# Layer 0 of a fused four-layer kernel: VectorE's order, one stored copy of q*v for even images, unpadded blocks, and GpSimd on half of the product

## The chip, the cores and the metric

The kernel runs on one core of a Trainium2 chip. A core has TensorE (PE: matrix products, with a queue PEld for loading weights), VectorE (DVE), ScalarE (ACT), GpSimd (POOL), SyncE (SP, which here only issues DMAs) and 16 DMA engines. Each engine takes its own instructions in the order in which they stand, and waits at semaphores for the others. On-chip memory (SBUF) has 128 partitions; products arrive in PSUM, which has 8 banks. The metric is the device time in microseconds of one execution, as a median over runs.

## The reference

The whole reference is four layers on x of 8 images, 56 x 56 positions and 192 channels, each with a group norm ahead of it and a residual sum behind it. Only layer 0 matters here:

```python
p = silu(x @ p_w.T + p_b)
q = silu(x @ q_w.T + q_b)
v = silu(x @ v_w.T + v_b)             # 576 channels each
a1, a2 = mlp1(pos) * decay, mlp2(pos) * decay
qv = q * v
o1 = toeplitz(qv along w, a1)
o2 = toeplitz(qv along h, a2)
out = (p * (o1 + o2)) @ o_w.T + o_b
```

For each image and channel, `o1 + o2` is a product of q*v (56 x 56) with a Toeplitz matrix of 56 lags from the right, plus one with another Toeplitz matrix from the left. Both are done as one product whose summed dimension holds the rows of q*v and the rows of the Toeplitz matrix, alternately.

## The kernel before, in words

**Steps.** Layer 0 has two steps, and layers 1 to 3 follow. Step one is the loop over the images `for b in range(nimg)` with `layer0_in` and `layer0_qv`. Step two is `layer0_mix`, which multiplies with the Toeplitz rows and does the gate and the output projection. What passes from one to the other goes through two DRAM tensors, `left` and `right`. `left` holds q*v as (image, sub, h) rows of 56 x 64 (w, channel), `right` holds it as (image, sub, w) rows of (h, channel); a sub is 64 of the 576 channels. Behind q*v each holds the Toeplitz rows, 64 for each sub, of which the last 8 are zeros.

**Step one.** x lies as 128 partitions: 64 channels of one half of the image (s = 0) and 64 of the other (s = 1), three channel groups j and 1568 positions (`NH`) in each half. `layer0_in` takes the statistics (L157, twelve instructions an image), sums them over groups with two small matmuls (L176), takes a square root on ACT and normalises into `xn` (L371). `layer0_qv` goes over 14 tiles of 112 positions; for each, over two halves n of the channels (called half tiles here). A half tile is 12 matmuls (L387; in float32 each leaves two records, so 24), two sums with the bias on DVE (L393, from PSUM to `act`), two Silu on ACT (L394) and two products q*v on DVE (L395). `act` has 4 buffers, PSUM 4 tiles of two banks, `qv` 3 buffers. After both halves SP stores q*v: for each s one DMA to `left` (L398) and two to `right` (L403), all in pieces of 64 floats, 256 B.

**Between the tiles** the list `between[i]` runs other work: `coefs`, a generator that makes the Toeplitz coefficients in image 0 (L227 and on: two MLPs, small matmuls, DVE); `rows`, DMAs on ACT's queue that write the Toeplitz rows and the zero rows into `left` and `right` (L296, L301); `bias` and `masks` for layer 1 (bias table, L342 sums on DVE, DMAs on POOL's queue); `centred`, which prepares weights of layer 1 in image 2; and in tile 4 all of `layer0_in` of the next image.

**Order.** Nothing in step one is pinned: the framework's scheduler puts the instructions of each engine in an order by its own estimate of times, and may move work of a later image ahead of an earlier one.

**Step two.** For each image and sub a block is loaded by `layer0_block` (L417): `lt` and `rt`, 128 partitions of 56 x 64 floats, in which q*v rows and Toeplitz rows alternate; two buffers each, so the next block's load starts when the last but one is copied out. `layer0_operand` (L425) copies 8 or 16 channels out of it at a time: `lc` on POOL, `rc` on DVE and ACT in turn. `layer0_products` (L433) does 16 (or 8) small products from them: a group. A block is four groups (or eight smaller ones). In between, the gate (`layer0_gate`, L445 to L474; `layer0_gate_last`) of the preceding channels runs: projection p, Silu, transposes of o, product and output projection. One image is nine blocks.

Of the kernel before, what the change touches and what calls it, by code (L numbers as in the profile page):

```python
# [18 lines left out]
NT = H * W  # L19
# [43 lines left out]
NH = NT // 2  # L63
NTH = NH // TT
# [25 lines left out]
def kernel(ctx: ExitStack, tc: tile.TileContext, a: dict, out: bass.AP):  # L90
# [45 lines left out]
    none = dram.tile([QR], F32, name="none")  # L136
    left, right = (dram.tile([(nimg * W + 64) * NSUB, QR], F32, name=n) for n in ("left", "right"))
    qv_row = lambda b, s: (b * NSUB + s) * W
    toep_row = lambda s: nimg * NSUB * W + 64 * s
    x1 = [dram.tile([C, NT], F32, name=f"x1_{b}") for b in range(nimg)]  # L140
# [86 lines left out]
    def toeplitz_rows(psum, pool, rows):  # L227
# [62 lines left out]
        zero = pool.tile([128, QR // 128], F32, name="zero", bufs=1)  # L290
        nc.gpsimd.memset(zero, 0.0)
        nc.scalar.dma_start(none.rearrange("(p n) -> p n", p=128), zero)
        parts = [z[toep_row(0):].rearrange("(s k) n -> k s n", k=64) for z in (left, right)]
# [6 lines left out]
        def zeros(i, k):  # L300
            nc.scalar.dma_start(parts[i][k], none.partition_broadcast(NSUB))  # L301

        rows += [lambda i=i, k=k: zeros(i, k) for i in range(2) for k in range(W, 64)]
# [54 lines left out]
    def layer0_in(b, x, pool, psum):  # L358

        sc, sh = scsh[:, 0, b:b + 1], scsh[:, 1, b:b + 1]  # L360
        st = pool.tile([128, 3, NTH, 6], F32, name="gh_st")
        for t in range(NTH):
            gn_piece(st, x, t)
        mv = pool.tile([128, 1, 2], F32, name="gh_mv")
        gn_aggregate(st, mv[:, 0])
        run(gn_finish(mv, sc, sh, pool, psum, "qv"))
        xn = pool.tile([128, 3, NH], F32, name="xn0")
        n = NH if b else TT
        for t in range(NH // n):
            ts = bass.ts(t, n)  # L370
            nc.vector.tensor_scalar(xn[:, :, ts], x[:, :, ts], sc, sh, ALU.mult, ALU.add)  # L371
        return xn

    def layer0_qv(b, xn, pool, psum, w_qv, b_qv, between):

        lv, rv = (
            z[qv_row(b, 0):qv_row(b, 0) + NSUB * W].rearrange("(s h) (w d) -> s h w d", h=W, d=64) for z in (left, right)
        )
        for i in range(PH):
            qv = pool.tile([2 * W, 2, D1], F32, name="qv", bufs=3)  # L380
            for n in range(2):
                ns = slice(n * D1 // 2, (n + 1) * D1 // 2)
                ps = [psum.tile([2 * W, 2, 512], F32, name=f"qv{s}", tag="qv") for s in range(2)]
                for which in range(2):
                    for j in range(3):
                        for s in range(2):
                            nc.tensor.matmul(  # L387
                                ps[s][:, which, 0:D1 // 2], xn[64 * s:64 * s + 64, j, bass.ts(i, 2 * W)],
                                w_qv[64 * s:64 * s + 64, j, which, ns], start=(j == 0), stop=(j == 2),
                            )  # L390
                for s in range(2):
                    act = pool.tile([2 * W, 2, D1 // 2], F32, name="act", bufs=4)
                    nc.vector.tensor_tensor(act, ps[s][:, :, 0:D1 // 2], b_qv[:, :, ns], ALU.add)  # L393
                    nc.scalar.activation(act, act, AF.Silu)  # L394
                    nc.vector.tensor_tensor(qv[:, s, ns], act[:, 0], act[:, 1], ALU.mult)  # L395
            for s in range(2):
                h0 = H // 2 * s + 2 * i
                nc.sync.dma_start(  # L398
                    lv[:, h0:h0 + 2].rearrange("s h w d -> (h w) s d"),
                    qv[:, s].rearrange("t (s d) -> t s d", d=64),  # L400
                )
                for r in range(2):
                    nc.sync.dma_start(  # L403
                        rv[:, :, h0 + r].rearrange("s w d -> w s d"),
                        qv[r * W:(r + 1) * W, s].rearrange("w (s d) -> w s d", d=64),
                    )
            for step in between[i]:
                step()
# [1275 lines left out]
```

## Time and profile before

The profile is of one execution. Step one runs from about 28 to 849 us, step two to about 2050, layers 1 to 3 after that.

| what | value |
|---|---|
| median of 3 runs | 5769.45 us (5760.73 to 5771.72) |
| the profiled execution | 5770.6 us, its span 5768.8 us |
| busy over the span | PE 5181.2 us (90%), DVE 3336.5, ACT 2169.1, POOL 1420.2 |
| mean granted PE clock | 0.957 |
| `left` stores (L398) | 224 DMAs of 252 KB |
| `right` stores (L403) | 448 DMAs of 126 KB |
| block loads (L417) | 72 of `lt` and 72 of `rt`, 1792 KB each |
| DVE's q*v (L395) | 448 x 455 ns |
| ACT's Silu (L394) | 448 x 683 ns |
| DVE's normalisation (L371) of images 1 to 7 | 7 x 2729 ns |
| POOL's copies `lc` of 16 channels (L425) | 256 x 1936 ns |

How to read it: "busy" is the time in which an engine works on something, "records" are instructions as the profiler saw them. A group of instructions is named by line, engine, operation and tiles, then count, busy time, mean duration, and the idle time just before it with the name of what ended it. A view of stretches gives the busy time of each engine in that piece of the span; PE's clock in it is a share of the full one.

### The profile page before, as it was taken

The page shows a single profiled execution, that of the slowest core. Times are in us where ns is not written, and L with a number is a line of the kernel's source. Part 1 is how long each engine was busy: PE and PEld are TensorE (multiplying, and loading weights), DVE is VectorE, ACT ScalarE, POOL GpSimd, SP SyncE. Part 2 cuts the span into 40 slices and gives each one's busy share as a digit, 9 for nine tenths or more (in the row PEclk, how much of TensorE's full clock was granted, in tenths as well). Part 3 has the DMA queues.
Part 4 walks back from the last instruction along what each step waited for, and adds up shares of the span by engine and source line. Part 5 has one row for each costly group of instructions (what it writes and reads, how often), then busy time and mean ns, then how long its engine had stood idle before and what let it go on. Part 6 is the DMA issues. An engine that isn't in the chain of part 4 may idle for free. (4 is left out here: it accounts for less than half of the span.)

```text
span 5768.8 us, 116138 instructions
## 1 busy us (share of the span) xinstructions
PE 5181.2 (90%) x50342; PEld 3376.1 (59%) x50342; DVE 3336.5 (58%) x4710; ACT 2169.1 (38%) x2908; POOL 1420.2 (25%) x1107
## 2 busy tenths in 40 slices
PE   6898998999899979999997989999788798999999
PEld 4568765666666645555554657676344597444444
DVE  5777774555555546566665868888778202433331
ACT  2333443333333423333332004555476400433333
POOL 2100004444444424433342013333101101100100
PEclk8999999999999989999998989999899899999999
DMA  6888986776677633222222866666687598212211
GB/s 179 204 211 216 206 182 258 264 264 258 247 262 264 222 92 82 69 75 76 69 65 76 260 235 218 227 232 209 160 232 215 222 328 295 78 62 77 76 41 26
DMA packets 721922, 1013.94 MB, mean 176 GB/s; under 512 B 486376, under 2 KB 645444, under 8 KB 694644
## 3 DMA queue, kind: packets, MB, share of 16 engines
q1 hardware_dynamic: 706352, 940.12, 52.4%
q0 software_dynamic: 8512, 40.62, 2.1%
q10 hardware_dynamic: 6548, 25.78, 1.4%
q8 instruction: 396, 6.49, 0.5%
q14 instruction: 114, 0.93, 0.0%
HBM read 676.92 MB, written 345.97 MB: 177 GB/s over the span
## 5 line engine op out<-in xcount | busy, mean ns | idle before, releaser
L387 PE MATMUL qv<-w_qv_sb,xn 64*112 64x288 f32 x5376 | 711.3, 421 | 48.6 <-DVE act L393 45.4
L425 POOL COPY lc<-lt 128x896 f32<-128x896 f32 (+1 forms) x320 | 552.5, 1751 | 640.9 <-PE op L433 543.1
L387 PEld LDWEIGHTS qv<-w_qv_sb,xn 64*112 64x112 f32 x5376 | 558.5, 182 | 195.5 <-DVE act L393 58.1
L394 ACT ACTIVATE act<-act 112x576 f32<-112x576 f32 x448 | 300.6, 683 | 466.8 <-DVE act L393 427.4
L433 PE MATMUL op<-rc,lc 128*56 128x56 f32 x9216 | 339.1, 221 | 102.1 <-POOL lc L425 64.9
L433 PEld LDWEIGHTS op<-rc,lc 128*56 128x56 f32 x9216 | 307.8, 135 | 177.9 <-POOL lc L425 103.5
L1289 PE MATMUL ph<-y,w_sb 64*128 64x392 f32 x2304 | 397.7, 497 | 6.5 <-ACT hid L1293 6.5
L1300 PE MATMUL po<-hid,w_sb 128*64 128x392 f32 x2304 | 386.3, 494 | 0.0
L393 DVE TENSOR_TENSOR act<-qv,b_qv 112x576 f32<-112x576 f32 x448 | 320.7, 752 | 92.7 <-PE qv L387 92.4
L1307 DVE TENSOR_TENSOR x<-x,z 128x392 f32<-128x392 f32 x96 | 67.0, 698 | 524.2 <-ACT z L1305 524.2
L425 ACT COPY rc<-rt 128x896 f32<-128x896 f32 (+1 forms) x160 | 256.3, 1606 | 249.7 <-PE op L433 227.2
L805 PE MATMUL qk_ps<-xr,wg 64*96 64x392 f32 x1536 | 334.2, 538 | 1.8 <-DVE xr L752 1.7
L1016 PE MATMUL cv<-zc,wt 128*128 128x224 f32 x1536 | 313.6, 356 | 24.2 <-DMA zc<-pd 24.2
L1016 PEld LDWEIGHTS cv<-zc,wt 128*128 128x128 f32 x1536 | 291.0, 190 | 67.5 <-issue 51.2
L1289 PEld LDWEIGHTS ph<-y,w_sb 64*128 64x128 f32 x2304 | 220.0, 188 | 175.9 <-issue 25.5
L445 PE MATMUL pj<-xn,w_p_sb 64*128 64x392 f32 x1536 | 309.8, 511 | 12.4 <-DVE xn L533 8.2
L1190 PE MATMUL cps<-zc,wt 128*128 128x224 f32 x1536 | 300.2, 356 | 18.2 <-DMA zc<-zd 16.8
L1190 PEld LDWEIGHTS cps<-zc,wt 128*128 128x128 f32 x1536 | 289.6, 189 | 28.7 <-issue 21.3
L466 PE MATMUL y<-pp,w_o_sb 128*64 128x392 f32 x1536 | 285.9, 501 | 4.8 <-DVE x L474 4.1
L459 DVE TENSOR_TENSOR pp<-pp,ot 128x784 f32<-128x784 f32 x128 | 124.2, 970 | 284.8 <-ACT pp L450 272.9
L1300 PEld LDWEIGHTS po<-hid,w_sb 128*64 128x64 f32 x2304 | 162.7, 137 | 213.8 <-issue 213.8
L1031 POOL TENSOR_TENSOR rows<-rows,loc 128x896 f32<-128x896 f32 x96 | 220.8, 2300 | 261.7 <-ACT rows L1027 201.9
(233 smaller groups left out, 8895.1 us busy)
## 6 DMA issues: line engine op xcount, KB each, us to landing
lt<-left SPq DMA_DIRECT2D x72, 1792.0 KB
rt<-right SPq DMA_DIRECT2D x72, 1792.0 KB
left<-qv SPq DMA_DIRECT2D x224, 252.0 KB
right<-qv SPq DMA_DIRECT2D x448, 126.0 KB
wt<-in_band_dram SPq DMA_DIRECT2D x23, 2048.0 KB
wt<-in_band_dram SPq DMA_DIRECT2D x11, 4096.0 KB
zc<-pd SPq DMA_DIRECT2D x187, 232.0 KB
pd<-pt SPq DMA_DIRECT2D x7, 5568.0 KB
```

What stands on the lines that cost most here:

```text
L387: nc.tensor.matmul(ps[s][:, which, 0:D1 // 2], xn[64 * s:64 * s + 64, j, bass.ts(i, 2 * W)], w_qv[64 * s:64 * s + 64, j, which, ns], start ...
L393: nc.vector.tensor_tensor(act, ps[s][:, :, 0:D1 // 2], b_qv[:, :, ns], ALU.add)
L394: nc.scalar.activation(act, act, AF.Silu)
L425: copy(c[:, 0:nu], raw.rearrange("p (w u d) -> p u d w", u=nu, d=64 // nu)[:, :, d0:d0 + 8])
L433: nc.tensor.matmul(op[64 * u:64 * u + W, i, :], lc[:, u, i], rc[:, u, i], start=True, stop=True)
L445: nc.tensor.matmul(ps[0:M, s, 0:TT], w_p[64 * s:64 * s + 64, j, d0:d0 + M], xn[64 * s:64 * s + 64, j, ts], start=(j == 0), stop=(j == 2),)
L466: nc.tensor.matmul(y[64 * s:64 * s + 64], w_o[0:M, c, 64 * j:64 * j + 64], pp[0:M, s], start=(c == gated[0][0]), stop=(c == gated[-1][0]),)
L805: nc.tensor.matmul(in_pairs(ps[s]), wg[64 * s:64 * s + 64, j, c0:c0 + HC], in_slots(xr[64 * s:64 * s + 64], (3 * g + j) * GW), start=(j == ...
L1016: nc.tensor.matmul(dst, wt[:, c4 + i, 128 * q:128 * q + 128], zc[:, :, c4 + i, q:q + NPAIR], start=(q == 0), stop=(q == 1),)
L1190: nc.tensor.matmul(dst.rearrange("p (b n) -> p b n", n=NPAIR), wt[:, c4 + i, q * OP:(q + 1) * OP], zc[:, :, c4 + i, q:q + NPAIR], start=(q ...
L1289: nc.tensor.matmul(ps[:, s, 0:TT], w0[64 * s:64 * s + 64, j, m * 128:(m + 1) * 128], y[64 * s:64 * s + 64, j, ts], start=(j == 0), stop=(j ...
L1300: nc.tensor.matmul(ps[64 * s:64 * s + 64], w1[:, m, 64 * j:64 * j + 64], hid[:, m, s], start=(m == 0), stop=(m == 5),)
```

## The change

- **DVE in source order.** A manual schedule for DVE is entered before step one's loop, so that DVE's instructions stand as the program writes them. The first step of `coefs` is drawn ahead of the first `layer0_in`.
- **`layer0_in` is a generator.** It yields between statistics, the group sums and the normalisation; the loop draws one step after each of the tiles 3 to the last but one. Normalisation is done in four pieces, for image 0 on DVE and for the others on POOL.
- **`layer0_qv`**: even images have 13 tiles (twelve of 120 positions and one of 128), odd ones the 14 of 112. The products q*v of a half tile are written down after the bias sums of the next one; s = 0 on DVE and s = 1 on POOL.
- **Stores**: q*v of every image goes to `left`; only odd images also go to `right`, which is half as large.
- **Blocks**: `lt` and `rt` take 112 partitions, 56 rows of each kind in alternation, without the 8 pad rows. For an odd image `rt` comes from `right` as before. For an even one the Toeplitz rows come from `right` in one DMA and q*v from `left` in another, which turns (h, w) into (w, h) in pieces of 256 B.
- The zero rows and their 16 DMAs are gone.

```diff
+QT = [[(120 * i, 120) for i in range(12)] + [(1440, 128)], [(112 * i, 112) for i in range(14)]]
...
-    left, right = (dram.tile([(nimg * W + 64) * NSUB, QR], F32, name=n) for n in ("left", "right"))
+    left, right = (dram.tile([n * NSUB, QR], F32, name=z) for n, z in ((nimg * W + 64, "left"), (nimg // 2 * W + 64, "right")))
+    right_row = lambda b, s: 64 * NSUB + qv_row(b // 2, s)
...
-        rows += [lambda i=i, k=k: zeros(i, k) for i in range(2) for k in range(W, 64)]
...
+        xn = pool.tile([128, 3, NH], F32, name="xn0")
+        yield xn
         for t in range(NTH):
             gn_piece(st, x, t)
+            yield
         mv = pool.tile([128, 1, 2], F32, name="gh_mv")
         gn_aggregate(st, mv[:, 0])
-        run(gn_finish(mv, sc, sh, pool, psum, "qv"))
+        for _ in gn_finish(mv, sc, sh, pool, psum, "qv"):
+            yield
+        yield
+        for t in range(NTH):
+            ts = bass.ts(t, TT)
+            eng = nc.gpsimd if b else nc.vector
+            eng.tensor_scalar(xn[:, :, ts], x[:, :, ts], sc, sh, ALU.mult, ALU.add)
+            if t % 2:
+                yield
...
+        def multiply(i, t0, M, n, qv, acts):
+            ns = slice(n * D1 // 2, (n + 1) * D1 // 2)
+            for s in range(2):
+                eng = (nc.vector, nc.gpsimd)[s]
+                eng.tensor_tensor(qv[0:M, s, ns], acts[s][0:M, 0], acts[s][0:M, 1], ALU.mult)
+            for s in range(2 * n):
+                nc.sync.dma_start(
+                    bass.AP(one.tensor, one.offset + 64 * (NH * s + t0), [[64, M], [64 * NT, NSUB], [1, 64]]),
+                    qv[0:M, s].rearrange("t (s d) -> t s d", d=64),
+                )
+                for r in range(2 * (b % 2)):
+                    nc.sync.dma_start(
+                        rv[:, :, H // 2 * s + 2 * i + r].rearrange("s w d -> w s d"),
+                        qv[r * W:(r + 1) * W, s].rearrange("w (s d) -> w s d", d=64),
+                    )
+
+        for i, (t0, M) in enumerate(QT[b % 2]):
...
                 for s in range(2):
-                    act = pool.tile([2 * W, 2, D1 // 2], F32, name="act", bufs=4)
-                    nc.vector.tensor_tensor(act, ps[s][:, :, 0:D1 // 2], b_qv[:, :, ns], ALU.add)
-                    nc.scalar.activation(act, act, AF.Silu)
-                    nc.vector.tensor_tensor(qv[:, s, ns], act[:, 0], act[:, 1], ALU.mult)
+                    nc.vector.tensor_tensor(acts[s][0:M], ps[s][0:M, :, 0:D1 // 2], b_qv[0:M, :, ns], ALU.add)
+                for s in range(2):
+                    nc.scalar.activation(acts[s][0:M], acts[s][0:M], AF.Silu)
+                if later:
+                    later.pop()()
+                later.append(lambda now=(i, t0, M, n, qv, acts): multiply(*now))
...
+        x = left[qv_row(b, s):qv_row(b, s) + W]
+        twos = lambda one, delta: bass.AP(one.tensor, one.offset, [[QR, W], [delta * QR, 2], [1, QR]])
+        nc.sync.dma_start(raw[0][0:2 * W], twos(x, toep_row(s) - qv_row(b, s)))
+        rows_t, rows_x = 64 * s, right_row(b, s)
+        if b % 2:
+            nc.sync.dma_start(raw[1][0:2 * W], twos(right[rows_t:rows_t + W], rows_x - rows_t))
+        else:
+            nc.sync.dma_start(raw[1][0:2 * W:2], right[rows_t:rows_t + W])
             nc.sync.dma_start(
-                t, bass.AP(one.tensor, one.offset, [[QR, 64], [(odd - even) * QR, 2], [1, QR]]),
+                raw[1][1:2 * W:2].rearrange("w (h d) -> w h d", d=64), x.rearrange("h (w d) -> w h d", d=64)
             )
...
+        st.enter_context(tc.manual_schedule(engines={mybir.EngineType.DVE}))
+        next(coefs)
+        ahead = layer0_in(0, x, pool, psum)
+        xn = next(ahead)
+        run(ahead)
...
+                ahead = layer0_in(b + 1, x, pool, psum)
+                xn_next = next(ahead)
+                for i in range(3, len(QT[b % 2]) - 1):
+                    between[i].append(lambda: next(ahead, None))
             layer0_qv(b, xn, pool, psum, w_qv, b_qv, between)
-            xn = ahead[0] if ahead else None
+            run(ahead)
+            xn = xn_next
```

## The prediction

> **What bounds the kernel now.** First the groups of instructions by cost, for step one (q, v and q*v of the eight images) and step two (the products with the Toeplitz rows).
>
> ```profile
> L387 PE MATMUL qv<-w_qv_sb,xn 64*112 64x288 f32 x5376 | 711.3, 421 | 48.6 <-DVE act L393 45.4
> ...
> L393 DVE TENSOR_TENSOR act<-qv,b_qv 112x576 f32<-112x576 f32 x448 | 320.7, 752 | 92.7 <-PE qv L387 92.4
> ...
> L433 PE MATMUL op<-rc,lc 128*56 128x56 f32 x9216 | 339.1, 221 | 102.1 <-POOL lc L425 64.9
> ```
>
> Step one's products start at 28.6 us and its last activation is at 848.6: 820 us. Step two reads what step one left in DRAM, and its products start at 854, so a microsecond gained in step one is gained at the end. Second, the busy time in stretches of 20 us: span, PE, PEld, DVE, ACT and POOL busy (with instructions), granted clock, DMA share, GB/s.
>
> ```profile
> 60.00:80.00 20.00, 11.81 (x64) 7.94 (x66) 15.25 (x35) 4.06 (x6) 0.00 (x0) 0.67 0.64 153
> ...
> 500.00:520.00 20.00, 20.00 (x168) 20.00 (x166) 15.69 (x28) 9.45 (x14) 0.00 (x0) 1.00 0.97 220
> ...
> 540.00:560.00 20.00, 10.83 (x65) 10.14 (x63) 12.52 (x25) 3.72 (x7) 0.00 (x0) 0.74 0.66 179
> ...
> 620.00:640.00 20.00, 17.98 (x133) 13.30 (x131) 15.15 (x28) 9.78 (x14) 0.00 (x0) 0.91 0.96 237
> ...
> 760.00:780.00 20.00, 20.00 (x170) 14.81 (x168) 16.17 (x28) 9.44 (x14) 0.00 (x0) 1.00 0.87 178
> ```
>
> Undisturbed, PE does 168 records in 20 us, 8.4 per us, at clock 1.00: 5376 records would take 640 us. The other 180 us are the stretches like 60 and 540, with 64 or 65 records and a lowered clock. Third, why: the timeline at such a place.
>
> ```profile
> 211.82 1.51 DVE L157 BATCH_NORM_STATS2 gh_st<-x 128x6 f32<-128x392 f32 x3 [6.15 <-DMA x<-in_x_dram]
> 213.24 0.74 DVE L393 TENSOR_TENSOR act<-qv,b_qv 112x576 f32<-112x576 f32 x1
> ...
> 214.03 0.24 PEld L325 LDWEIGHTS bp<-raw,rev 49*49 49x49 f32 x2 [5.62 <-DVE act L393]
> ...
> 243.50 1.73 DVE L342 TENSOR_TENSOR bmt<-mk,bt 128x196 f32<-128x196 f32 x6 [3.92 <-DMA bmask<-bmt]
> ```
>
> DVE runs its queue in order. The scheduler has put statistics of a later image, and mask sums, ahead of the bias sums (L393) that free PSUM; they wait for a DMA, and PE waits behind them. So step one is bounded by PE, with stalls made by DVE's order. Last, step two, in stretches of 10 us:
>
> ```profile
> 1160.00:1170.00 10.00, 6.99 (x182) 5.09 (x178) 7.21 (x12) 5.52 (x6) 9.76 (x5) 1.00 0.90 352
> 1170.00:1180.00 10.00, 7.59 (x102) 4.17 (x102) 7.37 (x9) 4.48 (x4) 6.60 (x4) 0.83 0.97 373
> ...
> 1270.00:1280.00 10.00, 10.00 (x96) 6.60 (x93) 4.51 (x6) 2.36 (x3) 0.97 (x1) 1.00 0.01 2
> ```
>
> Here PE is nearly full, but in about half of each image's 149 us (1192 us over 8) the DMA engines are at 0.8 to 1.0 (1160 to 1190 and 1200 to 1260); in the densest part, 1160 to 1190, loads and POOL's copies set the pace.
>
> **Part 1, fewer tiles.** An even image goes from 14 token tiles to 13. A tile is 48 records, so 4 x 48 = 192 go, and 5184 at 8.4 per us take 617 us: -23 us on the path. The price per record is that of the 288 streamed columns; 120 rows in place of 112 lengthen only the weight load (173 ns at the median, 185 by rows), which is hidden (14.8 of 20 us).
>
> **Part 2, DVE in source order.** Per half tile DVE now has two bias sums (2 x 752) and one q*v (455 ns): 1.96 of PE's 2.86 us. Between tiles come at most three statistics (3 x 554 = 1.66 us) or six mask sums (6 x 356 = 2.1). PSUM holds two half tiles, so the two sums of one (1.5 us) must end within PE's 2.86 us on the next, and may be 1.4 us late; 1.96 + 2.1 - 2.86 = 1.2 fits. What stays:
> - The group-norm chain of seven images. The late stretch 620 to 640 has little else and lacks 35 records, 4.2 us: 7 x 4.2 = 29.
> - Other small matmuls: bias, means, Toeplitz and mask rows, 18 us of the 24.7 us that step one has outside L387.
> - Image 0: the two MLP rounds now stand between tiles, and PE waits for DVE behind two sums and a product, some 3.3 us each: 7. The ACT queue's wait for the coefficients (8.4 us in the waits, less 2.9 slack): 5.
> - Image 2: the four weight scalings, 2.1 us beside the statistics: 2. DVE now asks for the positions before the first statistics; it ran that at 22.6 us unhindered, and x came at 17.0, so the start moves by 0 to 6; I take 2.
> Sum 617 + 29 + 18 + 12 + 4 = 680.
>
> **Part 3, POOL.** POOL's half of q*v is not in the trace at this size. From 448 columns (936 ns) and 1176 (2188 ns), 288 make 661 ns; by the slower 896-column row (2300 ns) 740. Either fits 2.86 us. The normalisation of 1568 columns takes 1.84 us and 196 columns 0.52, so 1176 take 1.46, and four in a row 5.8. The built order puts all four (in the later images two and two, or three and one) ahead of a product; DVE's sum two half tiles on waits for that product to free `act`. POOL: 3.0 + 5.8 + 0.7 = 9.5 us after the half tile's end, against 8.6 when the sum could start: 0.9 late, within 1.4. In image 0 POOL also issues 42 small DMAs at 617 ns, 9 and 16 of them between products: products 2 to 5 come up to 4 us late; I add 4. So step one takes 684 us, -136, and 2 are lost at the start (counted above). Bounds: no stall left, 617 + 25 = 642, -178; half of the present stalls kept (820 - 640 - 25 = 155), 719, -101. I say -136, as its own error 15 us either way.
>
> **Part 4, DMAs.** Even images store once: half their packets go. The sixteen zero-row DMAs go from ACT's queue; they stood beside a loaded PE and are worth nothing by themselves. The odd images keep 0.87 to 0.97 of the engines, as now. The first gather stands in SP's queue between image 0's stores and image 1's and waits for the former to land; three `qv` buffers (17 us) cover it.
>
> In step two every even block (36 of 72) loads 56 whole Toeplitz rows and gathers 3136 pieces of 256 B. No row shows such a read. Cheapest: as whole rows, 0.8 MB at 430 GB/s (1230 to 1234 us), 1.9 us. Nearest: the stores of the same piece, 0.87 x 16 engines x 20 us over 3.56 MB, 20 ns a piece, 3.9 us. Dear: twice that, 7.8. With the left rows and the Toeplitz half (2.4 MB, 5.6 us) a block needs 7.5, 9.5 or 13.4 us, against 8.5 now (3.67 MB). I take the nearest, +1.0. It counts in the half of the time that is at the DMA's limit: 18 x 1.0 = +18 us; bounds -18 and +88.
>
> The Trainium skill, "DMA: Bandwidth & Descriptors", section "Why a DMA increments its semaphore by 16 and not by 1", speaks against counting the dropped pad rows as a gain: a copy uses the largest number of engines up to 16 that divides both sides' slowest dimensions, so 56 and 112 make 14 engines of 8 rows, where 64 and 128 made 16 of 8. By that rule an even block's load would be an estimated 10.9 us and my +18 would be +43; no run here shows it yet.
>
> **Part 5, PE's order in step two.** In the built program odd images keep their order. In even ones the products stand in runs of four to twelve groups where they were mixed one to three at a time with the gate's matmuls. In a run POOL's copy (1.94 us) outlasts the 16 products (32 x 36.8 ns = 1.18), 0.76 us a group beyond the two ready; some 15 more such groups an image make 11 us at most and 0 at least. I take 3, since the same gate work stands between the runs: +12.
>
> **Sum.** -136 + 2 + 18 + 12 = -104 on the profiled execution's 5770.6 us (span 5768.8) makes 5666.6; that execution is 1.2 us above the median of the three runs, 5769.45, so **5665 us**.
>
> **Rivals.**
> - *The gather is hidden.* SP issues a block ahead, and the DMA rests from 1260 to 1280. Step two as now, step one -150: 5620. Against: 0.97 to 1.00 at the dense part.
> - *The in-order queues pass on their waits.* DVE, POOL and `act` now form one ring, so any late link stops PE. If each of seven chains costs 10 us instead of 4.2 and image 0 another 20: 5665 + 41 + 20 = 5726. For it: POOL's small DMAs. Against: DVE's 0.9 us of rest per half tile.
> - *The gather becomes step two's bound.* With x ns a piece, 18 blocks lose 0.196x - 2.9 us each; with the 12 of the order, that eats 134 at x = 49 ns, and from there the kernel is slower. At 60 ns: 160 + 12 - 134, 5808 us. For it: strided reads of 256 B, unseen here. Against: stores of 6272 B run at 201 GB/s (1194 to 1198) and those of 256 B at 178, so the piece's size costs little.
> - *The order does nothing.* DVE waits for something else. Against: each stall above names its DMA. Then only -23 + 30 is left, 5776.
>
> **How the numbers follow.** The forecast 0.60 (its own range 5630 to 5705), hidden gather 0.16, passed-on waits 0.13, gather as bound 0.09, order without effect 0.02. The range 5605 to 5735 takes in the first three. This kernel's measurement can't tell 0.2%, 11.5 us, from no change. Faster 0.87, same 0.03, slower 0.10.
>
> **What would show it.** Step one's products ending near 712 us, at 165 to 168 records per 20 us outside seven short dips; no statistics waiting for x ahead of a bias sum. A gather of 4 to 5 us, and even images in step two 4 to 10 us longer than odd ones. Wrong: DVE's bias sums waiting for POOL, or PE waiting in even images for `rc` behind the gather.

## The result, and the profile after

The changed kernel takes 5979.25 us (median of 4 runs, 5971.93 to 5992.76), the one before 5767.22 beside it: a ratio of 1.0371, 95% interval 1.035 to 1.0393. It is 212 us slower; 5665 had been forecast, and the range ended at 5735.

The two profiled executions differ by 208.5 us of span, and three boundaries split this:

| stretch | before | after | change |
|---|---|---|---|
| start to step two's first product | 854.3 | 774.9 | -79.4 |
| step two, first to last product | 1198.2 | 1521.7 | +323.5 |
| from there to the end (nothing edited) | 3716.3 | 3680.7 | -35.6 |

The forecast had -134 in the first row, +30 in the second and nothing in the third. So of the 312 us between its -104 and the +208.5, step two makes 293 and step one, with the start, 55; layers 1 to 3 give 36 back.

The groups by cost, POOL's copies before and then the groups after (in each line: busy us, mean ns, then the idle time before it and who ended most of it):

```profile
L425 POOL COPY lc<-lt 128x896 f32<-128x896 f32 (+1 forms) x320 | 552.5, 1751 | 640.9 <-PE op L433 543.1 <-DMA lt<-left 62.7 <-PE ot L456 19.8
...
L405 PE MATMUL qv<-w_qv_sb,xn 64*112 64x288 f32 (+2 forms) x5184 | 675.2, 415 | 16.8 <-DVE act L411 12.5 <-DVE xn L369 3.2 <-DVE ct L288 0.8
L441 POOL COPY lc<-lt 112x896 f32<-112x896 f32 (+1 forms) x320 | 522.2, 1654 | 990.7 <-PE op L449 810.0 <-DMA lt<-left 172.8 <-PE y L482 7.3
L449 PE MATMUL op<-rc,lc 112*56 112x56 f32 x9216 | 385.1, 241 | 243.0 <-POOL lc L441 126.0 <-DVE rc L441 90.5 <-issue 15.4
L441 DVE COPY rc<-rt 112x896 f32<-112x896 f32 (+1 forms) x160 | 178.8, 1139 | 161.6 <-DMA rt<-left 70.9 <-DMA rt<-right 67.0 <-PE op L449 23.8
```

In step one PE's wait for the bias sums fell from 45.4 to 12.5 us: that part works. In step two PE's idle time before products went from 102.1 to 243.0, and POOL and DVE wait for loads: 172.8 us for `lt` alone, 62.7 before. Stretches of step two, the first line before and the others after, with busy time by engine, granted clock, DMA share and GB/s:

```profile
1230.00:1234.00 4.00, 4.00 (x32) 2.51 (x31) 2.33 (x3) 2.57 (x2) 0.78 (x1) 1.00 1.01 430
...
1000.00:1010.00 10.00, 8.36 (x128) 5.51 (x128) 4.21 (x4) 3.94 (x4) 5.72 (x4) 0.70 0.89 201
1080.00:1090.00 10.00, 7.82 (x130) 4.99 (x129) 5.09 (x7) 4.22 (x4) 3.44 (x2) 1.00 0.90 201
1090.00:1100.00 10.00, 4.91 (x57) 3.22 (x55) 1.45 (x2) 2.27 (x3) 3.42 (x2) 0.91 0.87 196
...
1130.00:1140.00 10.00, 10.00 (x99) 6.88 (x96) 4.10 (x5) 3.32 (x4) 1.92 (x2) 1.00 0.00 0
```

The lines after lie in an odd image, with plain loads and no gather. The DMA engines are busy at 0.9 and move 201 GB/s, where the program before moved 430. They are as busy (0.84 to 0.98) from 980 to 1120 us; then they are idle for part of the time, as in the last line, and PE is full. What a load of 56 and 56 rows runs at is the first thing that the prediction had not asked.

The x of each image is stored when its last gate ends; the distance between these stores is the time of an image. Before it is 149 to 152 us; after, 203 for the even images (201.2, 207.4, 200.3) and 179 for the odd ones (183.9, 171.8, 180.8). So both kinds lose. How the loss is shared out between them is less sure: such a store comes 40 to 50 us into the next image, not always at the same place. From an image's first product to the next one's, the even images after take 195 us and the odd ones 187 (151 and 149 before).

The same image 1, from first product to first product, before and after:

```profile
1006.00:1155.00 149.00, 136.28 (x1896) 91.35 (x1893) 82.59 (x104) 58.42 (x58) 69.13 (x40) 0.99 0.69 256
...
975.00:1167.00 192.00, 151.93 (x1888) 101.32 (x1884) 78.03 (x104) 58.55 (x58) 64.73 (x40) 0.87 0.78 177
```

PE waits 27 us more in it, and is also busy 16 us longer with the same work, at a granted clock of 0.87 in place of 0.99. Whether the lower clock comes from the waits was not tried.

Step one, first to last product, takes 735.9 us instead of 817.8; the forecast's 684 ran to the last Silu, which is 682 to the last product. Many of its stretches are full (168 records in 20 us from 540 to 560, 620 to 640 and 700 to 720), others are not. One of the places is this; SP's queue in order of time (start, length):

```profile
329.75 4.26 SPq L387 DMA_DIRECT2D left<-qv  x3
334.18 1.71 SPq L427 DMA_DIRECT2D lt<-left  x2
335.94 19.21 SPq L387 DMA_DIRECT2D left<-qv  x4
```

and POOL in the same stretch:

```profile
344.63 0.79 POOL L385 TENSOR_TENSOR qv<-act 112x288 f32<-112x288 f32 x1 [2.07 <-ACT act L413]
356.03 1.07 POOL L385 TENSOR_TENSOR qv<-act 112x288 f32<-112x288 f32 x1 [10.61 <-DMA left<-qv]
```

The `lt` halves of step two's first two blocks are loaded here, 1.6 MB each. The stores of `qv` behind them land late, POOL waits 10.6 us for a free `qv`, and the ring of DVE, ACT and POOL stands. An earlier place is in image 0, where ACT's queue holds the first DMA of the Toeplitz rows, and that one waits for the coefficients to land in DRAM:

```profile
111.94 0.68 ACT L413 ACTIVATE act<-act 120x576 f32<-120x576 f32 x1 [13.28 <-DMA coef<-ct]
...
113.65 0.56 PE L177 MATMUL gh_m<-gh_mv,gmath_sb 128*128 128x1 f32 x2 [9.58 <-DVE gh_mv L161]
```

### The profile page after: what moved, and what is told of

It is laid out like the page before. It is cut to its first block, busy times and chain, and to the rows that moved or that the text cites. A ratio compares the mean times of both kernels' runs of the same rounds, so it can differ in the third digit from the quotient of the medians.

```text
span 5977.3 us, 115317 instructions
## 1 busy us (share of the span) xinstructions
PE 5255.9 (88%) x50150; PEld 3399.1 (57%) x50150; DVE 3196.8 (53%) x4455; ACT 2151.8 (36%) x2892; POOL 1605.9 (27%) x1350
## 5 line engine op out<-in xcount | busy, mean ns | idle before, releaser
L441 POOL COPY lc<-lt 112x896 f32<-112x896 f32 (+1 forms) x320 | 522.2, 1654 | 990.7 <-PE op L449 810.0
L405 PE MATMUL qv<-w_qv_sb,xn 64*112 64x288 f32 (+2 forms) x5184 | 675.2, 415 | 16.8 <-DVE act L411 12.5
L405 PEld LDWEIGHTS qv<-w_qv_sb,xn 64*112 64x112 f32 (+2 forms) x5184 | 517.6, 182 | 164.5 <-DVE act L411 22.9
L449 PE MATMUL op<-rc,lc 112*56 112x56 f32 x9216 | 385.1, 241 | 243.0 <-POOL lc L441 126.0
L449 PEld LDWEIGHTS op<-rc,lc 112*56 112x56 f32 x9216 | 350.4, 154 | 322.0 <-POOL lc L441 170.3
L413 ACT ACTIVATE act<-act 112x576 f32<-112x576 f32 (+2 forms) x432 | 286.0, 682 | 432.5 <-DVE act L411 385.4
L411 DVE TENSOR_TENSOR act<-qv,b_qv 112x576 f32<-112x576 f32 (+2 forms) x432 | 306.7, 751 | 213.7 <-PE qv L405 193.3
L441 ACT COPY rc<-rt 112x896 f32<-112x896 f32 (+1 forms) x160 | 255.3, 1596 | 416.7 <-PE op L449 290.6
L461 PE MATMUL pj<-xn,w_p_sb 64*128 64x392 f32 x1536 | 339.6, 536 | 33.5 <-ACT pp L466 23.1
L1206 PE MATMUL cps<-zc,wt 128*128 128x224 f32 x1536 | 299.1, 356 | 18.7 <-DMA zc<-zd 17.0
L385 POOL TENSOR_TENSOR qv<-act 112x288 f32<-112x288 f32 (+2 forms) x216 | 178.4, 827 | 464.7 <-ACT act L413 373.5
```

The costliest lines, as they stand in the source:

```text
L405: nc.tensor.matmul(ps[s][0:M, which, 0:D1 // 2], xn[64 * s:64 * s + 64, j, t0:t0 + M], w_qv[64 * s:64 * s + 64, j, which, ns], start=(j == ...
L411: nc.vector.tensor_tensor(acts[s][0:M], ps[s][0:M, :, 0:D1 // 2], b_qv[0:M, :, ns], ALU.add)
L413: nc.scalar.activation(acts[s][0:M], acts[s][0:M], AF.Silu)
L441: copy(c[:, 0:nu], raw[0:2 * W].rearrange("p (w u d) -> p u d w", u=nu, d=64 // nu)[:, :, d0:d0 + 8])
L449: nc.tensor.matmul(op[64 * u:64 * u + W, i, :], lc[:, u, i], rc[:, u, i], start=True, stop=True)
L461: nc.tensor.matmul(ps[0:M, s, 0:TT], w_p[64 * s:64 * s + 64, j, d0:d0 + M], xn[64 * s:64 * s + 64, j, ts], start=(j == 0), stop=(j == 2),)
```

## The experiments

Three measures serve throughout: *one*, step one from its first to its last product; *two*, step two from its first to its last; and the mean time of an even and of an odd image by the stores of x (the first interval counts as odd, the last is left out). The last column has the same from first product to first product, for images 1 to 6. Where the two differ, the total *two* decides.

| run | kernel us | ratio to before [95%] | one | two | even / odd by stores | even / odd by first products |
|---|---|---|---|---|---|---|
| before | 5767 | 1 | 817.8 | 1198.2 | 151 / 150 | 151 / 149 |
| changed kernel | 5979 | 1.0371 [1.035, 1.0393] | 735.9 | 1521.7 | 203 / 179 | 195 / 187 |
| e1_pad_loads | 5804.7 | 1.0084 [1.0052, 1.0115] | 714.5 | 1362.7 | 189 / 153 | 191 / 152 |
| e2_store_twice | 5723.7 | 0.9943 [0.9927, 0.9959] | 765.9 | 1208.4 | 151 / 151 | 152 / 151 |
| e3_before_unpadded | 6057.6 | 1.0523 [1.0491, 1.0555] | 815.7 | 1489.2 | 188 / 185 | 188 / 185 |
| e4_pad_gather | 5779.7 | 1.0036 [1.0022, 1.005] | 714.5 | 1344.2 | 185 / 156 | 188 / 153 |
| e5_no_pool_half | 5808.1 | 1.0082 [1.0053, 1.0111] | 735.7 | 1327.4 | 184 / 151 | 185 / 149 |
| e6_dve_scheduled | 5849.4 | 1.0151 [1.0126, 1.0177] | 776.8 | 1346.6 | 185 / 156 | 189 / 153 |
| e7_pe_source_order | 5769.1 | 1.0015 [1.0005, 1.0025] | 715.8 | 1320.6 | 168 / 164 | 169 / 163 |
| e8_changed_pe_order | 6024.5 | 1.0458 [1.0442, 1.0473] | 736.1 | 1549.6 | 199 / 191 | 199 / 191 |
| e10_late_group_sum | 5776.4 | 1.003 [1.0017, 1.0043] | 719.1 | 1319.8 | 168 / 164 | 170 / 162 |
| e11_pe_order_step_one | 5775.7 | 1.0027 [1.0018, 1.0036] | 720.9 | 1319.7 | 168 / 163 | 169 / 163 |
| e12_late_x_load | 5728.3 | 0.9951 [0.9933, 0.9969] | 714.5 | 1276.5 | 160 / 158 | 163 / 155 |
| e14_twice_source_order | 5771.5 | 1.0025 [1.0014, 1.0037] | 770.0 | 1261.8 | 157 / 158 | 156 / 159 |
| e15_fine_gate | 5781.7 | 1.0035 [1.0022, 1.0049] | 724.1 | 1336.8 | 170 / 164 | 171 / 163 |

**The loads' shape.** e1 gives the changed kernel the loads of 128 partitions back (`lt`, and `rt` of odd images), with the zero rows that these read and nothing multiplies (their 16 DMAs stand on ACT's queue again, as in the kernel before):

```diff
-        twos = lambda one, delta: bass.AP(one.tensor, one.offset, [[QR, W], [delta * QR, 2], [1, QR]])
-        nc.sync.dma_start(raw[0][0:2 * W], twos(x, toep_row(s) - qv_row(b, s)))
+        twos = lambda one, delta: bass.AP(one.tensor, one.offset, [[QR, 64], [delta * QR, 2], [1, QR]])
+        nc.sync.dma_start(raw[0], twos(x, toep_row(s) - qv_row(b, s)))
...
-            nc.sync.dma_start(raw[1][0:2 * W], twos(right[rows_t:rows_t + W], rows_x - rows_t))
+            nc.sync.dma_start(raw[1], twos(right[rows_t:rows_t + W], rows_x - rows_t))
```

> The changed kernel, but every block load that interleaves two kinds of rows (lt always, rt for odd images) again takes 64 rows of each kind into 128 partitions; the last 16 partitions are loaded and not used, and the zero rows are written again. The gather for even images and its 56 Toeplitz rows stay. Theory A (the load of 56 + 56 rows into 112 partitions moves at 201 GB/s where that of 64 + 64 moved at about 430, so loads set step two's pace): odd images fall back to about 149 us, even ones to between 149 and 175, step two from 1528 us to 1200 to 1300, the kernel to 5660 to 5760. Theory B (the 256 B gather and the bunched order of PE in even images cost the time): next to nothing, above 5900. Theory C (DMA queueing on SP because of a third DMA per block): above 5900 too.

e2 is e1 with every image stored twice in 14 tiles, as before, so without a gather:

```diff
-QT = [[(120 * i, 120) for i in range(12)] + [(1440, 128)], [(112 * i, 112) for i in range(14)]]
+QT = [[(112 * i, 112) for i in range(14)]] * 2
...
-        if b % 2:
+        if True:
```

> As e1_pad_loads, and every image stores q*v twice again and has 14 tiles of 112, so no gather is left: step two is that of the kernel before, step one has DVE in source order, the spread group norm and POOL's half of q*v. Theory A and B alike: step two 1190 to 1200 us. Step one: 14 tiles of 48 records in each image are 640 us against 617, the first block loads are short again, so about 750 us against the 737 of the changed kernel and the 820 of the one before: the kernel near 5695. If step one's gain came from the halved stores rather than from the order, step one stays above 800 and the kernel above 5740.

e3 is the opposite: the kernel before with nothing changed but its block loads, 56 and 56 rows into 112 partitions.

```diff
-            one = z[even:even + 64]
+            one = z[even:even + W]
             nc.sync.dma_start(
-                t, bass.AP(one.tensor, one.offset, [[QR, 64], [(odd - even) * QR, 2], [1, QR]]),
+                t[0:2 * W], bass.AP(one.tensor, one.offset, [[QR, W], [(odd - even) * QR, 2], [1, QR]]),
```

> The kernel before, with nothing changed but the block loads: 56 + 56 rows into 112 partitions instead of 64 + 64 into 128. Theory A: a block's two loads take 16 us at 201 GB/s instead of 8.5, step two grows by 200 to 300 us, the kernel to 5970 to 6070. Theories B and C: step two unchanged or a little shorter (12.5% fewer bytes), 5740 to 5770.

The shape alone costs the old program 301 us (6057.6 against 5756.4 beside it), 291 of them in step two: 12.5% fewer bytes, and every image 35 to 37 us longer. Its step two, stretches and waiting groups:

```profile
1242.00:1248.00 6.00, 1.85 (x38) 1.11 (x38) 4.79 (x8) 2.11 (x2) 0.81 (x1) 1.00 0.88 191
1262.00:1268.00 6.00, 0.43 (x6) 0.00 (x0) 1.75 (x3) 0.19 (x1) 0.97 (x1) 0.77 0.91 194
```

```profile
L425 POOL COPY lc<-lt 112x896 f32<-112x896 f32 (+1 forms) x320 | 520.5, 1642 | 964.0 <-PE op L433 743.2 <-DMA lt<-left 208.7 <-PE y L466 11.9
L433 PE MATMUL op<-rc,lc 112*56 112x56 f32 x9216 | 386.2, 240 | 280.8 <-POOL lc L425 159.5 <-DVE rc L425 99.0 <-ACT rc L425 15.0
```

The same picture as in the changed kernel, without any of its other parts. e1 repairs the odd images (153 us) and shortens step one by a further 21 us; it missed its expectation by 45 us, because even images stay at 189. The 21 us are not the block loads alone. From 40 to 120 us e1 has 446 of step one's product records and the changed kernel 372, and from 40 to 320 us 1884 and 1790: 94 records, 11 us at 8.4 per us, are lost before the first block load is issued at 334 us. In e1 a DMA of zero rows, which needs no coefficients, stands at the head of ACT's queue there, and the wait of 13.28 us shown above is absent; that this makes the difference is read from the queue and was not tried by itself. So the loads among the stores can have at most the other 10.

e2, which has no gather and plain loads, has 151 everywhere and is 0.6% faster than the kernel before. Its step one came out at 765.9 where about 750 was expected, and step two at 1208.4 where 1190 to 1200 was.

**What a load costs by its shape.** Two kernels with DMAs alone.

> No layer is computed; only DMAs on SP, four of a shape at a time and each shape alone, out is a copy of x. In order: 64 partitions; 128; 64 + 64 interleaved; 56 + 56 interleaved; 112 plain rows; 48 + 48; 64; 48 at partition 64; 56 on every other partition; 64 on every other; the gather of 56 x 56 pieces of 256 B to every other partition; the same with 64 x 56; the gather to 56 neighbouring partitions; 120 plain rows; then stores of q*v pieces with 112, 120 and 128 partitions, and the pair of 56. Theory A (engine count 14 and eight neighbouring partitions per engine): 56 + 56 near 200 GB/s and DMA share 0.88, 64 + 64 near 430. If the rate goes with the partitions reached, 64 partitions also give near 200, and 112 plain rows something between. Gather: 20 ns a piece and 14 engines make 4.5 us for 0.8 MB (180 GB/s); at twice that 90 GB/s.

> Only DMAs, no layer is computed: fourteen load shapes, six of each, with a full stop between the shapes (m1_load_shapes let them overlap). Theory: full speed (about 430 GB/s) belongs to loads whose rows spread over all 128 partitions in steps that divide 128 (128 rows, 64 on every other, 32 on every fourth, perhaps 64 in partitions 32 to 95), half speed to 64 in partitions 0 to 63, and 56, 56+56, 112 and 96 rows lie at 170 to 260. Rival, the count of rows alone decides (a multiple of 16 rows is fast, others slow): then 96 and 112 rows and 64 rows in partitions 0 to 63 run at 430 too, and only 56 is slow. Two loads of 64 rows to partitions 0 to 63 and 64 to 127: 430 if neighbours in the queue overlap, 206 if not.

In both, neighbouring shapes still overlap at their borders, so the times below are the spacings in the middle of each group in the second kernel (a row is 14336 B). For the 56 + 56 rows the spacing is too long, since the stretch shown below moves more than they do, 183 GB/s: loads of the next shape take part in it.

| load | us | GB/s |
|---|---|---|
| 128 rows; 64 + 64 rows alternating | 4.28; 4.29 | 429; 428 |
| 64 rows on every other partition | 2.14 | 429 |
| 32 rows on every fourth | 1.1 | 417 |
| 56 + 56 rows alternating (the change's) | 10.1 | 159 |
| 112 rows in order; 96 rows in order | 7.4; 8.0 | 217; 172 |
| 64 rows in partitions 0 to 63 | 4.44 | 207 |
| 56 rows on every other partition | 3.84 | 209 |
| partitions 0 to 63 and 64 to 127 as two loads | 8.16 | 225 |
| gather of 64 columns; of 56 | 4.2; 4.8 | 218; 167 |

The stretches of the second kernel for 128 rows, 56 + 56, 112, 64 in order, and 64 on every other partition (DVE and POOL busy, clock, DMA share, GB/s):

```profile
70.00:84.00 14.00, 0.88 (x8) 0.00 (x0) 1.00 1.00 428
128.00:150.00 22.00, 0.44 (x4) 0.00 (x0) 1.00 0.99 183
190.00:215.00 25.00, 0.66 (x6) 0.00 (x0) 1.00 0.98 219
270.00:280.00 10.00, 0.59 (x5) 0.00 (x0) 1.00 1.01 206
358.00:364.00 6.00, 0.59 (x5) 0.00 (x0) 1.00 0.99 418
```

The DMA engines are full in all five: with the wrong shape they are as busy and move about half. The stretch of 56 + 56 moves 183 GB/s, which is 8.8 us a load, and the stretches of the kernels 201, which is 8.0; so such a load takes 8.0 to 10.1 us, 1.9 to 2.4 times the 4.28 of the padded one. The first theory holds in kind (its 170 GB/s for the slowest shape was a little high by the spacings, and 64 rows in partitions 32 to 95 came 2.0 to 4.9 us apart, which settles nothing); the rival, by the count of rows alone, falls with 96 rows and 64 in order.

A block before was two loads of 4.28 us, 8.6; after it is 16.0 to 20.2 in an odd image and 16.6 to 18.7 in an even one (8.0 to 10.1, + 3.84 + 4.8). At the kernel's own 201 GB/s nine odd blocks make 144 us. That is the 140 us, 980 to 1120, for which the DMA engines are busy in image 1: there loads are the bound. In the rest of the image PE works on with the gate. In the kernel before, nine blocks were 77 us of an image's 149.

**Gather or order.** e4 takes e1 and widens the even `rt` to 64 and 64 rows; the extra eight are never read.

```diff
-            nc.sync.dma_start(raw[1][0:2 * W:2], right[rows_t:rows_t + W])
+            nc.sync.dma_start(raw[1][0:128:2], right[rows_t:rows_t + 64])
...
-                raw[1][1:2 * W:2].rearrange("w (h d) -> w h d", d=64), x.rearrange("h (w d) -> w h d", d=64)
+                raw[1][1:128:2].rearrange("w (h d) -> w h d", d=64), bass.AP(x.tensor, x.offset, [[64, 64], [QR, W], [1, 64]]),
```

> As e1_pad_loads, but an even image's rt is loaded as 64 Toeplitz rows on every other partition and 64 gathered columns on the others, instead of 56 and 56; the 8 extra rows of each are never read. The order of instructions on PE, DVE and POOL is the same as in e1_pad_loads, only DMAs differ. Theory A, the loads' price sets step two: from m1_load_shapes, 64 Toeplitz rows take 2.15 us instead of 3.9 and a gather of 64 columns 4.2 instead of 4.9, so an even block needs 10.6 us instead of 13.1; over 36 blocks 88 us less: images 0, 2, 4 and 6 about 170 us between x stores instead of 190, kernel 5705 to 5735 us. Theory B, the bunched order of PE in even images sets their time: even images stay at 185 to 190, kernel 5790 to 5805.

An even block now loads in 10.6 us instead of 13, and even images go from 189 to 185 only, the 185 to 190 of theory B (the kernel, at 5779.7, lies between the two ranges). Two stretches in an even image, and POOL's copies there:

```profile
1184.00:1192.00 8.00, 7.22 (x44) 3.84 (x44) 3.20 (x4) 1.64 (x2) 0.00 (x0) 1.00 0.01 2
1192.00:1200.00 8.00, 5.98 (x32) 2.63 (x31) 2.31 (x3) 1.89 (x3) 0.00 (x0) 1.00 0.00 0
1200.00:1208.00 8.00, 6.18 (x139) 4.75 (x140) 2.37 (x3) 3.77 (x4) 4.65 (x3) 1.00 0.01 2
```

```profile
1165.79 6.77 POOL L450 COPY lc<-lt 112x896 f32<-112x896 f32 x4 [20.25 <-PE op L458]
1203.35 11.70 POOL L450 COPY lc<-lt 112x896 f32<-112x896 f32 x6 [30.79 <-PE op L458]
```

For 16 us the DMA moves nothing and POOL does nothing, while PE works through gate matmuls; then products come in a run and PE waits for most copies, 0.5 to 1.4 us each and once 5.9. The two kinds of work no longer cover each other: in image 2 of e4 (1090 to 1280 us) PE waits 10.2 us for `lc` and 8.4 for `rc`, and in the gate 6.2 for `pp` before `y` and 5.5 before `pj`; in image 3 (1280 to 1432) it is 5.4 and 3.0, and next to nothing in the gate. In the trace the products of an even image stand in 19 runs of up to eight groups, where those of an odd image stand in 35 runs of one to four. It is so in the changed kernel, e1 and e4, which have the gather; in e2, which has none, even images have 35 runs too. e7 takes PE's order from the source in step two:

```diff
+        st.enter_context(tc.manual_schedule(engines={mybir.EngineType.PE}))
         ops = [psum.tile([128, 8, H], F32, name=f"op{k}", bufs=1) for k in range(2)]
```

> As e4_pad_gather, with PE in source order in step two: groups of products and pieces of the gate alternate in even images as in odd ones; DMAs are those of e4_pad_gather. Theory B, the bunched order is what even images lose in e4_pad_gather (184 us between x stores against 153 for odd ones): they come down to 150 to 158, step two to 1215 to 1240 us, the kernel to 5650 to 5680 us. Theory A, the gather's own time at the DMA is what they lose: they stay at 175 or more and the kernel at 5750 or more. Odd images have plain loads in both and show whether the source order costs anything by itself.

Even images fall to 168, but odd ones rise to 164, so neither expectation was met. SP's queue and DVE in an odd image of e7 show why:

```profile
1297.38 2.55 SPq L436 DMA_DIRECT2D lt<-left  x1
1309.42 0.33 SPq L553 DMA_DIRECT2D x<-in_x_dram  x1
1309.85 0.55 SPq L439 DMA_DIRECT2D rt<-right  x1
```

```profile
1326.36 1.78 DVE L450 COPY rc<-rt 112x896 f32<-112x896 f32 x2 [11.18 <-DMA rt<-right]
```

SP stands 10 us at the load of the next x, whose buffer is still being stored, and the block behind it is late. e12 issues that load after the second pass; e14 does both in e2, where no gather runs:

```diff
                     xn = normed(b, x[b])
-                    if b + 1 < nimg:
-                        x.append(load(b + 1))
+                if g == 1 and b + 1 < nimg:
+                    x.append(load(b + 1))
```

> As e7_pe_source_order, with the load of the next image's x issued after the second pass of an image instead of the first, where its buffer is free. In e7_pe_source_order SP's queue stands 12 us at that load in every image, the block load behind it comes late and PE waits 12 us for DVE's rc. Theory: that wait is the price of the source order; all images lose 10 to 12 us, odd ones to 152 to 155, even ones to 156 to 160, kernel 5680 to 5705 us. Rival: the block load is late for another reason and PE finds the next wait: within 20 us of e7_pe_source_order.

> As e2_store_twice (no gather, every load of 128 partitions), with PE in source order in step two and the late load of x as in e12_late_x_load: it shows what the source order costs when no gather runs. Theory, a gather of 64 columns costs little once the order is right: even and odd images within 5 us of those of e12_late_x_load. Rival, the gather itself costs: even images here 10 us or more below those of e12_late_x_load.

With one order everywhere, even images take 160 us with the gather (e12) and 157 without (e14); step two as a whole is 14.7 us longer, 3.7 for each of four images (by first products even images are 6 us longer and odd ones 4 shorter). So the gather itself costs 3 to 4 us an even image, as e14's theory had it. The order costs more: of e4's 185 the source order alone takes away 17 (e7), with the late load of x 25 (e12). That load is no part of the order, and SP waits for it in e4 too; e4 with the late load was not built, so 17 to 25 is as far as the runs go. The load of x was about half of what the source order costs; at 157 to 158 an image is still 7 us above the scheduler's order (151 in e2). e12 came 23 us above its expectation, and the 7 us an image would more than cover that; it is 0.5% faster than the kernel before all the same. e15 cuts the gate's pieces finer, in search of those 7 us:

```diff
                 nc.scalar.activation(pp[0:M], ps[0:M, :, 0:TT], AF.Silu, bias=vec("p_b", c, M))
+                yield
...
             nc.scalar.activation(pp, ps[:, :, 0:TT], AF.Silu, bias=vec("p_b", c))
+            yield
```

> As e12_late_x_load, with the gate's pieces cut once more (behind each projection's Silu), so that in step two at most six products' runs of 8 matmuls stand together, most two. It is meant as the version that keeps one stored copy, the gather, DVE's order and POOL's half. Theory: PE's waits in step two (rc 71, lc 41, o 18 us in e12_late_x_load) are products standing too close together; images come to 149 to 155 us, kernel 5665 to 5700 us. Rival: the transposes then stand too late before the next product and DVE's queue is the bound: images stay at 158, kernel 5720 to 5740.

Both its theory and its rival missed: images take 164 to 170, PE waits more for `rc` (81.6 against 71.1 us between 900 and 2000) and for DVE's `o` (27.2 against 18.0).

e8 puts the line of e7 into the changed kernel itself, with its slow loads:

> The changed kernel with nothing but PE in source order in step two; its loads stay those of 56 and 56 rows. Theory, the slow loads set the pace of every image and hide most of the order's price: odd images stay near 180 to 186 us, even ones come from 201 to 185 to 190 (e3_before_unpadded, with slow loads and the old order, had 186), kernel 5900 to 5940 us. Rival, the order costs in the changed kernel what it costs at full speed of the loads, some 30 us an even image: even images near 170, kernel 5850 us.

Missed: step two is 28 us longer, and the kernel 45 us slower still. By the stores even images gain 4 us and odd ones lose 12; by first products both lose 4. While loads set the pace, the source order buys nothing here.

**Step one.** e5 and e6 take parts out of e4, whose step two isn't in question here. e5 gives both products to DVE, e6 leaves out the manual schedule of DVE.

```diff
-                eng = (nc.vector, nc.gpsimd)[s]
+                eng = nc.vector
```

```diff
-        st.enter_context(tc.manual_schedule(engines={mybir.EngineType.DVE}))
         next(coefs)
```

> As e4_pad_gather, but both products q*v of a half tile are on DVE; POOL keeps the normalisation. DVE then has 2 x 752 + 2 x 455 = 2.41 us of work per half tile against PE's 2.86. Theory: DVE still fits, POOL's half buys little, and step one changes by -10 to +15 us against e4_pad_gather. Rival 1: POOL's half is needed, since DVE with statistics and mask sums falls behind: step one +25 us or more. Rival 2: POOL as a third link passes on the waits of the stores (its waits for left and right stores were 85 us in the changed kernel): step one 15 us or more shorter.

> As e4_pad_gather, but without the manual order of DVE in step one: the scheduler places DVE's instructions, as before. Theory: DVE's order is what made step one shorter, so step one ends 40 to 80 us later than in e4_pad_gather and the waits of bias sums behind statistics and mask sums are back. Rival: the fewer tiles and fewer stores made it shorter, and the order does little: within 15 us of e4_pad_gather.

Without DVE's order step one is 62 us longer. Its waits on PE and on DVE, in us, times and longest:

```profile
PE qv L414 <- DVE act L420: 50.7, 14, 9.8
...
DVE gh_st L160 <- DMA x<-in_x_dram: 52.5, 6, 11.5
```

Both are the waits that the prediction named, and in e4 the first is 7.4 us and the second is absent. POOL's half is worth 21 us: neither the expectation nor its rivals had that size quite right. e10 and e11 are e7 with more done about PE's waits at the group sums: one `yield` more behind the statistics, and then PE's source order in step one too (the manual schedule there takes in PE).

```diff
         gn_aggregate(st, mv[:, 0])
+        yield
         for _ in gn_finish(mv, sc, sh, pool, psum, "qv"):
```

> As e7_pe_source_order, with one more yield between a group norm's statistics and its first group sum, so that in four of seven chains the matmul gh_m stands 10 to 24 records later on PE. Theory: PE's waits for gh_mv (43 us over 8 images in e4_pad_gather) are PE reaching gh_m before DVE's queue does; where it stands later they shrink, step one 10 to 25 us shorter. Rival: the wait is set by the length of the chain, not by PE's place: within 5 us.

> As e10_late_group_sum, with PE in source order in step one too, so that every gh_m stands a whole tile behind its statistics. Theory: all the waits for gh_mv go, step one 25 to 45 us shorter than in e7_pe_source_order. Rival: in image 0 the small matmuls of the Toeplitz coefficients now wait for DVE in PE's queue, and step one is longer by 10 us or more.

Neither helped: step one is 3 and 5 us longer than in e7. In e10 PE's wait for `gh_mv` went from 43 to 27 us, and 27 is image 0's, ahead of the first product: the waits in the loop were gone. But PE's wait for the bias sums rose from 7.8 to 22.4.

## Why the prediction was wrong, and where it was right

**The step that failed is Part 4's price of the block loads.** "With the left rows and the Toeplitz half (2.4 MB, 5.6 us)" took 430 GB/s from rows of 128-partition loads and used it for 56 and 56 rows. They run at 201 GB/s in the better stretches of the kernel and at 159 by their spacing in the kernel of loads: 8.0 to 10.1 us and 3.84 in place of 5.6, and an odd block's two loads, not priced at all since they only lost bytes, 16.0 to 20.2 in place of 8.6. Part 4 bounded the gather from both sides and gave the plain loads no bounds; a change of shape was taken for a change of size. e3 shows that this alone is worth +291 us of step two, where the forecast had +18 for all loads.

The estimate made there from the Trainium skill's rule ("DMA: Bandwidth & Descriptors", section "Why a DMA increments its semaphore by 16 and not by 1") pointed the right way and was too low: 14 engines of 16 made 10.9 us of an even block, and the shapes' own times make 16.6 to 18.7. The rule gives 96 rows all 16 engines, and these ran at 172 GB/s here.

Another page of the Trainium skill bears on it: "SBUF — State Buffer", section "Door 1: The DMA port swizzle (why `[64,N]` ≈ `[32,N]`)", says that a load's speed follows how many of 16 ports its partitions reach, and that 0 to 63 reach eight. Our 207 GB/s there, against 429 for the same 64 rows on every other partition, agrees. By its map 96 and 112 rows reach all ports too, and these ran at 172 and 217 here; the measurement decides, and why 112 partitions are slow stays open.

**Part 4's gather was right.** 4.8 us alone against the 3.9 taken and the 7.8 of the dear end, and 3 to 4 us an even image in e12 against e14 (forecast 18 us over four, 4.5). The rival with the gather as the bound had the right sign and the wrong transfer: a slower kernel came, but through the plain loads, so it was right by luck.

**Part 5 was too small by far.** It gave the bunched order 11 us an image at most and took 3. At full-speed loads it is 17 to 25 (e4 to e7 and e12). The step counted only POOL's copies outlasting the products of a run, which is the smaller part of PE's added waits (5 us for `lc` in e4's image 2 against 3), and not that in between, while POOL and the DMA stand still, the gate alone waits for its own ACT and DVE. In the changed kernel, as far as e8 shows, most of it lies behind the slow loads; that would be why the two prices, 291 and 70 to 100 for four images, come to more than the 323 measured.

**Part 1 and Part 2 had the mechanism right.** DVE's order is worth 62 us by itself (e6), and fewer tiles with fewer stores 51 (e2 to e4, 765.9 to 714.5); Part 1 had 23 for the tiles. The size was off: 682 forecast, 735.9 measured. Of these 54 us, 21 go in e1: at most 10 are the block loads in SP's queue, Part 4's error once more, and 11 are lost in image 0 and soon after. There Part 2 priced ACT's wait for the coefficients at 5 us, and it came to 13.28 on ACT and 9.58 on PE; Part 4 gave the zero-row DMAs no worth, and with them back at the head of that queue the wait is absent. With the 21 gone, 714.5 stand for 5184 records that need 617: 97 us lost where the prediction counted 65 (682 less 617). Image 0 has a large share: in e4, 476 records between 32.3 and 120 us, where 8.4 per us would make 737, so 31 us; Part 2 had 12.

**Part 3** had POOL's product at 661 ns, and it took 827 (the normalisation 1.44 us, as forecast). That it fits behind PE was right in the main, though DVE's bias sums waited 20.0 us for it in all (longest 2.3), which had been named as a sign of being wrong. Without POOL's half step one is 21 us longer (e5).

Of the signs that were to show it, full stretches came, but with more than seven dips between them, and step one's products ended at 769, not near 712; the gather of 4 to 5 us came. Even images were longer than odd ones by 24 us (by first products 8, inside the forecast's 4 to 10), but odd ones were themselves 29 to 38 longer than before. The other sign of being wrong came too: PE's wait for DVE's `rc` rose from 12.5 to 90.5 us, and `rc` waited as long for the plain loads (67.0) as for the loads of even images (70.9).

## What to carry to other kernels

Price a load by its shape, not by its bytes: dropping pad rows from a 128-partition load made it 12.5% smaller and about twice as long, so leave the pads in, or lay the rows out so that whatever is read beyond them may be read. When a DMA is added, look at what the scheduler makes of it on the engine that the DMA isn't on: here the gather cost 3 to 4 us an image and the new order of PE 17 to 25. The two versions that beat the kernel before, e2_store_twice at 0.9943 and e12_late_x_load at 0.9951, do so by about half a percent; they keep the reordered step one and the full-width loads; one that had the scheduler's order of odd images for even ones too was not built.

## What had not been expected of the hardware

The DMA engines show a share of 0.98 to 1.01 at 183 to 219 GB/s just as at 428: the share says that they are occupied, not that they deliver. Worked out from share and rate, a row of 14336 B occupied one of the 16 engines for 0.54 us in the kernel before (1.01 at 430 GB/s) and for 1.0 us after (0.89 at 201).

64 rows on every other partition take 2.14 us, 56 rows in the same way 3.84.

Layers 1 to 3, which nobody touched, were 35.6 us shorter in the changed kernel, 33 in e1, 36 in e4, 26 in e12 and 19 in e14, and within 8 us of before in e2 and e3. In the changed kernel the granted clock in the four 200 us stretches from 2519 on is 1.00, 1.00, 0.99 and 0.98; before, in those from 2275 on, 0.96, 0.97, 0.95 and 0.99. What sets it was not tried.
